# Attention tail of a fused two-layer kernel: a second level of Strassen's rule for four of seven value products, a moved transpose, and one accumulator tile in the MLP

## Chip, core and metric

The kernel runs on one core of one Trainium2 chip, in float32, as one launch. The metric is the device time of that launch in microseconds (us). The core has five engines with queues of their own, each of which works strictly through its queue: TensorE (PE in the profile, with its weight loads as PEld), VectorE (DVE), ScalarE (ACT), GpSimd (POOL) and SyncE (SP, which here only issues DMAs).

## What is computed

The reference chains two layers on x of shape (2, 512, 32, 32), that is two batches of 512 channels by 1024 positions.

```python
# layer 0: deformable attention (with a small MLP as position bias), then, for each batch
x = x + out_proj(attention) + out_b
h1 = gelu(mlp_w1 @ bn2(x) + mlp_b1)            # 512 -> 2048 channels
x = x + mlp_w2 @ h1 + mlp_b2                   # 2048 -> 512 channels
# layer 1: plain attention over the 1024 positions, one head of 512 channels
q, k, v = Wq @ x + bq, Wk @ x + bk, Wv @ x + bv
attn = softmax(q.T @ k / sqrt(512))            # 1024 x 1024
out = x + Wp @ (v @ attn.T) + bp
```

The change lies in the MLP of layer 0 (one tile) and at the end of layer 1.

## The kernel before

**Strassen's rule.** All large products are block products with seven multiplications instead of eight. Each operand is cut in four blocks; `fold` and `spread` (lines 116 to 128, on VectorE or POOL) form three more blocks from them by sums, so that a list of seven blocks stands for each operand. `PARTS` (line 112) says which two blocks each of the products 1 to 7 multiplies. `multiply` (line 130) takes a PSUM tile (128 x 2 x 512) for each product, lets TensorE fill it, and calls a function that takes it out of PSUM: a copy on ScalarE, or a sum on VectorE (`plus`, line 136, all of whose instructions carry the line L137).

**A second level.** `twice` (lines 141 to 178) does two of these products at once, each by seven half-sized steps: it is used in the first layer of the MLP. The order of its steps is written out by hand (`STEPS`, line 139: place in the order, number of the step); set g is shifted by 7 g places, and other work can be put in between as "fills", with a place of its own. In each step both products of the set write halves of one PSUM bank. Steps 1, 6, 7, 4 share a bank and add up in it, each after ScalarE has copied the state before out; step 2 has a bank in a second tile, whose other bank takes steps 5 and 3. VectorE takes steps 2, 5 and 3 out.

**PSUM.** In the MLP and the tail, `mq` deals four PSUM tiles in turn (line 1151). A product therefore can begin when the product four tiles earlier has been taken out.

**Stages.** Up to about 1900 us the kernel works through the position bias (L697 and what belongs to it). Then come the output projection, the MLP, and layer 1. The MLP has eight units (line 1152): batch 0 and 1, and in each four slices of the 2048 hidden channels. A unit is `layer1` (line 1056), with gelu on ScalarE, and `layer2` (line 1100), with seven products in the order 2, 1, 3, 5, 6, 7, 4. Products 1, 5, 6, 7 are collected over the four units of a batch in a tile `acc` of four quarters (line 1103): the first unit copies them there on ScalarE (L1108), the others add on VectorE. A new `acc` is taken for each batch from a pool that has room for one. `finish(b)` (line 1120) adds the four quarters to x in eight VectorE sums; that of batch 0 is issued behind layer 1 of batch 1's first unit (lines 1165 to 1167).

**The tail, layer 1.** It runs over the two batches (line 1196). Weights are merged beforehand: gg for q and k, gn for v and Wp together, loaded and folded on POOL by `load_g` (line 907); gn is loaded once, ahead of the loop. For each batch: seven products form q (line 1225), 2 x 7 form the scores of two halves u of the queries (`scores`, line 1249), each followed by a softmax. `turn(u, e)` (line 1272) transposes a half by 32 TensorE transposes, four ScalarE copies into aT (L1281), and three VectorE sums. Seven products `turned` (line 1295) form the transposed values vt. Seven products of vt by aT (line 1368, order 1, 2, 6, 7, 5, 3, 4, eight matmuls of 128 x 512 each) give the output; their results are added to x on VectorE, and each finished quarter is stored by two SP DMAs of 256 KB (L1331, L1366). The order on TensorE is: turn(0), the seven products for vt, turn(1), the seven products of vt by aT. At the end of the VectorE work on vt, `blocks(b + 1)` (line 924) prepares the next batch's x in four sums.

Instructions of all helpers carry the helper's line: L1201 are the matmuls of q, the scores and the value-times-attention products, L1299 those of vt, L1040 those of the MLP's plain products, L159 those of `twice`.

Of the kernel before, what the change touches and what calls it, by code (L numbers as in the profile page):

```python
# [8 lines left out]
F32 = mybir.dt.float32  # L9
AF = mybir.ActivationFunctionType  # L10
ALU = mybir.AluOpType
# [46 lines left out]
def conv_seq_kernel(ctx: ExitStack, tc: tile.TileContext, x, xt, kst, pst, cst, vec, wsm, outw, w1, w2, wl, wlt, brow, out):  # L58
# [79 lines left out]

    STEPS = ((0, 1), (1, 2), (3, 6), (4, 5), (6, 7), (9, 4), (12, 3))

    def twice(pool, sets, weights, moving, dest, done, fills=()):
        todo = [(7 * g + t, g, q) for g in range(len(sets)) for t, q in STEPS]
        todo += [(t, None, fill) for t, fill in fills]
        held = {}
        for _, g, q in sorted(todo, key=lambda e: e[0]):
            with tc.issue_after(newest(mybir.EngineType.PE)):
                if g is None:
                    q()
                    continue
                if q == 1:  # L150
                    held[g] = pool.tile([P, 2, 512], F32, tag="ps2", name="sw")
                if q == 2:
                    held[g, 2] = pool.tile([P, 2, 512], F32, tag="ps2", name="sw")
                bank = {2: lambda: held[g, 2][:, 0], 5: lambda: held[g, 2][:, 1], 3: lambda: held[g, 2][:, 1]}.get(
                    q, lambda: held[g][:, 0]
                )().rearrange("p (e n) -> p e n", e=2)
                s, t = PARTS[q]
                for e, p in enumerate(sets[g]):
                    nc.tensor.matmul(  # L159
                        bank[:, e, :], weights(p, s), moving(p, t), start=(q in (1, 2, 5) and e == 0), stop=True,  # L160
                        skip_group_check=True,
                    )
            d11, d12, d21, d22 = (dest(g, m, h) for m in range(2) for h in range(2))
            if q == 1:
                nc.scalar.copy(d11, bank)  # L165
            elif q == 2:
                plus(d11, d11, bank)
            elif q == 6:
                nc.scalar.copy(d12, bank)
            elif q == 7:  # L170
                nc.scalar.activation(d22, bank, AF.Copy, scale=-1.0)
                b5 = held[g, 2][:, 1].rearrange("p (e n) -> p e n", e=2)
                plus(d22, d22, b5, ALU.subtract)
            elif q == 4:
                nc.scalar.activation(d21, bank, AF.Copy, scale=-1.0)
            elif q == 3:
                plus(d12, d12, bank)
                done(g)
# [756 lines left out]
    with ExitStack() as top, tc.tile_pool(name="wp", bufs=1) as wp:  # L935
        halves = [(b, h) for b in range(B) for h in range(2)]
        units = [(b, p) for b in range(B) for p in range(NU)]
        wts, accs, copied = {}, {}, []

        def gather(w):  # L940
            for o, v in ((4, 2), (3, 0), (5, 4), (6, 5)):
# [114 lines left out]
        def layer1(p, we, w, xb, xe, hm, others=()):  # L1056
            def gelu(blk, src, scale=1.0):
                for m in range(2):
                    nc.scalar.activation(
                        hm[:, blk, m, :], src[:, m, :], AF.Gelu,  # L1060
                        bias=col("mb1", 4 * p + 2 * (blk // 2) + m), scale=scale,
                    )

            c11, c12, c21, c22, r5, r3 = (hm[:, j] for j in range(6))

            def weights(q, j):
                a = FIRST_W[PARTS[q][0]]
                return inner_w(w, we, a, a - 1)[j]

            def moving(q, j):  # L1070
                b_ = FIRST_X[PARTS[q][1]]
                return inner_x(xb, xe, b_, b_ - 1)[j]

            def dest(g, m, h):
                return hm[:, 2 * g : 2 * g + 2, m, 256 * h : 256 * h + 256]

            def done(g):
                if g == 0:
                    plus(c12, c12, c11)
                elif g == 1:  # L1080
                    plus(c22, c22, c12)
                    plus(c21, c21, c22)
                    gelu(2, c21, -1.0)
                else:
                    plus(c22, c22, r5)
                    gelu(3, c22, -1.0)
                    plus(c12, c12, r5)
                    plus(c12, c12, r3)
                    gelu(1, c12)

            def second():
                ps = mq.tile([P, 2, 512], F32, tag="ps2", name="sw")
                product(w, xb)(ps, 0, 0)
                plus(c11, c11, ps)
                gelu(0, c11)

            twice(mq, ((1, 6), (4, 7), (5, 3)), weights, moving, dest, done, ((21, second), *others))
            spread([hm[:, j] for j in range(7)])

        def layer2(b, p, w, hm):  # L1100

            if p == 0:
                accs[b] = mp.tile([P, 4, 2, 512], F32, tag="acc", name="acc")

            def own(j):
                a = accs[b][:, j]
                if p == 0:
                    return lambda ps: nc.scalar.copy(a, ps)  # L1108
                return lambda ps: plus(a, a, ps)

            def give(o2, h, op):
                x_ = xs[:, 2 * o2 : 2 * o2 + 2, b, h * 512 : (h + 1) * 512]
                return lambda ps: plus(x_, x_, ps, op)

            multiply(mq, (2, 1, 3, 5, 6, 7, 4), product(w, hm), {
                1: own(0), 5: own(1), 6: own(2), 7: own(3),
                2: give(0, 0, ALU.add), 3: give(0, 1, ALU.add), 4: give(1, 0, ALU.subtract),
            })

        def finish(b):  # L1120
            p1, p5, p6, p7 = (accs[b][:, j] for j in range(4))
            for o in range(NCH):
                nc.scalar.activation(xs[:, o, b, :], xs[:, o, b, :], AF.Identity, bias=col("mb2", o))
            v = [xs[:, o2 : o2 + 2, b, n : n + 512] for o2 in (0, 2) for n in (0, 512)]
# [19 lines left out]
        spread(op1[1])  # L1144
        project(1, *op1, op1w[:, 3:5].rearrange("p a k n -> p a (k n)"))
        xe, part = sums(xb)
        load_second(0)


# [40 lines left out]
    SC = float(C) ** (-0.5)  # L1190
    outv = out.rearrange("b (k p) n -> p k b n", p=P)
    with tc.tile_pool(name="sp", bufs=1) as sp:
        gn = sp.tile([P, 7, 2, 256], F32, name="gn")
        load_g(gn, 1)

        for b in range(B):
            def product(w, x, c=0, nk=2):
                def go(ps, a, b_):
                    for m in range(2):
# [72 lines left out]
            def turn(u, e):  # L1272
# [10 lines left out]
                            ps.rearrange("p a (c n) -> p a c n", n=P),  # L1283
                        )
                n = slice(256 * u, 256 * u + 256)
                spread([aT[:, j, :, n] for j in range(6)], range(3))

            e0 = scores(0)
            e1 = scores(1)
# [15 lines left out]
                return lambda ps: f(ps.rearrange("p a n -> p (a n)"))  # L1305

            def v5(ps):
                plus(vf[2], vf[2], ps, ALU.subtract)
                plus(vf[1], vf[1], ps)

            multiply(mq, (1, 6, 7, 4, 5, 3, 2), turned, {p: flat_(f) for p, f in {
                1: lambda ps: nc.scalar.copy(vf[0], ps), 6: lambda ps: plus(vf[1], vf[0], ps),
                7: lambda ps: nc.vector.scalar_tensor_tensor(vf[2], ps, -1.0, vf[1], ALU.mult, ALU.subtract),
                4: lambda ps: plus(vf[3], vf[2], ps, ALU.subtract), 5: v5,
                3: lambda ps: plus(vf[1], vf[1], ps), 2: lambda ps: plus(vf[0], vf[0], ps),
            }.items()})
            fold(nc.vector, vf)
            turn(1, e1)
            if b + 1 < B:
                xbl = blocks(b + 1)  # L1320


            x11, x12, x21, x22 = (xs[:, o : o + 2, b, n : n + 512] for o in (0, 2) for n in (0, 512))
            tv = sp.tile([P, 2, 512], F32, name="tv")
            for o in range(NCH):
                nc.scalar.activation(xs[:, o, b, :], xs[:, o, b, :], AF.Identity, bias=ub[:, 1, o : o + 1])

# [2 lines left out]
                for o in (2 * o2, 2 * o2 + 1):  # L1330
                    nc.sync.dma_start(out=outv[:, o, b, n], in_=xs[:, o, b, n])  # L1331

            def a1(ps):
                nc.scalar.copy(tv, ps)
                plus(x11, x11, ps)

            def a2(ps):
                plus(x11, x11, ps)
                store(0, 0)

            at = [aT[:, j] for j in (0, 1, 2, 3, 4, 5, 5)]

            def a6(ps):
                plus(tv, tv, ps)
                plus(x12, x12, tv)
                nc.vector.scalar_tensor_tensor(at[6], at[5], -1.0, at[2], ALU.mult, ALU.subtract)

            def a7(ps):
                plus(tv, tv, ps)
                plus(x22, x22, tv, ALU.subtract)  # L1350
                plus(x21, x21, tv, ALU.subtract)

            def a5(ps):
                plus(x22, x22, ps, ALU.subtract)
                store(1, 1)
                plus(x12, x12, ps)

            def a3(ps):
                plus(x12, x12, ps)
                store(0, 1)  # L1360

            def a4(ps):
                for m in range(2):
                    x_ = xs[:, 2 + m, b, 0:512]
                    plus(x_, x_, ps[:, m, :], ALU.subtract)
                    nc.sync.dma_start(out=outv[:, 2 + m, b, 0:512], in_=x_)  # L1366

            multiply(mq, (1, 2, 6, 7, 5, 3, 4), product(vt, at, nk=4), {
                1: a1, 2: a2, 6: a6, 7: a7, 5: a5, 3: a3, 4: a4,
            })  # L1370


def _constants(np):
# [113 lines left out]
```

## Time and profile before

| | |
|---|---|
| median of 3 runs | 2631.12 us (2630.61 to 2632.42) |
| the profiled execution | 2630.3 us, of which the profile's span is 2628.5 |
| granted TensorE clock, mean | 0.999 |
| TensorE, VectorE, ScalarE, POOL busy | 99%, 87%, 66%, 30% of the span |
| MLP, first step of `twice` to its last product | 1945.7 to 2319.6 us of the span |
| tail, batch 0 and batch 1 | 2319.6 to 2471.4, 2471.4 to 2628.5 us |
| last matmul's end, end of the span | 2623.3, 2628.5 us |

How to read the profile: a row of groups names line, engine, operation, output and input tiles, shape and count, then busy time and the mean duration of one in ns, then the idle time of the engine ahead of it and who ended it. A timeline row has the start and the duration of one instruction or of a run of equal ones (us), then engine, line, operation, tiles, count, and in brackets the idle time ahead of it. A float32 matmul is two MATMUL records. Starts of equal matmuls in a row are closer than their durations, since they are pipelined.

### The profile page before, as it was taken

How to read it: one execution, taken by the hardware profiler on the slowest of the kernel's cores; microseconds unless marked ns; L12 is line 12 of the kernel's file. 1: busy time of each engine (PE TensorE's matmuls, PEld its weight loads, DVE VectorE, ACT ScalarE, POOL GpSimd, SP SyncE). 2: the span in 40 equal slices, each digit the busy share in tenths (PEclk: the TensorE clock that was granted, in tenths of full speed). 3: DMA queues.
4: the chain of work that ended last, by engine and by line, in shares of the span. 5: the costliest groups of instructions: out<-in, count | busy, mean ns of one | idle time of the engine just before them, and what ended most of it. 6: DMA issues, size and time to landing. Idle time of an engine off the chain costs nothing.

```text
span 2628.5 us, 47874 instructions
## 1 busy us (share of the span) xinstructions
PE 2611.6 (99%) x19656; PEld 1005.9 (38%) x19656; DVE 2281.3 (87%) x1425; ACT 1742.8 (66%) x2311; POOL 798.3 (30%) x899
## 2 busy tenths in 40 slices
PE   9999999999999999999999999999999999999999
PEld 3333332333233333333333333333355655646454
DVE  7999999999999999999999999999785685666354
ACT  5887898878888878887887777777632242315041
POOL 1333333333333333333333333333333333200000
PEclk9999999999999999999999999999999999999999
DMA  5788878888877888888887888888777677300000
GB/s 190 177 176 183 188 167 173 184 181 195 176 172 170 180 177 197 175 176 173 174 185 168 183 172 173 179 176 178 172 189 159 143 169 160 71 16 0 32 1 32
DMA packets 164809, 403.52 MB, mean 154 GB/s; under 512 B 24784, under 2 KB 72032, under 8 KB 161904
## 3 DMA queue, kind: packets, MB, share of 16 engines
q0 software_dynamic: 99104, 256.29, 53.7%
q1 hardware_dynamic: 65056, 143.88, 15.6%
q8 instruction: 155, 2.54, 0.4%
q14 instruction: 62, 0.51, 0.1%
q10 hardware_dynamic: 432, 0.31, 0.0%
HBM read 81.10 MB, written 6.55 MB: 33 GB/s over the span
## 4 chain that ended last, share of the span: by engine, by line
PE 93%; DVE 3%; ACT 2%; issue 1%; DMA 0%; DVEq 0%; ACTq 0%
PE ps L697 65%; PE sw L1201 9%; PE sw L1040 6%; PE sw L159 5%; PE sw L987 2%; PE sw L1299 2%; PE sim L783 1%; PE psg L599 1%; DVE hm L137 1%; ACT rx L706 0%; DVE xs L137 0%; ACT ub L708 0%; PE pkv L533 0%; PE sim L766 0%; PE pt L800 0%
## 5 line engine op out<-in xcount | busy, mean ns | idle before, releaser
L697 PE MATMUL ps<-h,cw 128*32 128x512 f32 x16384 | 1776.3, 592 | 3.8 <-ACT rx L706 2.8
L680 DVE CUSTOM_DVE_ANT_1 h<-ta,tb 128x4096 f32<-128x4096 f32 (+1 forms) x257 | 1131.0, 4402 | 29.3 <-PE ps L697 26.4
L697 PEld LDWEIGHTS ps<-h,cw 128*32 128x32 f32 x16384 | 541.9, 110 | 1202.7 <-issue 1137.0
L706 ACT ACTIVATE rx<-ps,sc 128x1024 f32<-128x1024 f32 x512 | 568.0, 1109 | 145.4 <-PE ps L697 126.3
L708 ACT ACTIVATE ub<-ps,sc 128x1024 f32<-128x1024 f32 x256 | 308.2, 1204 | 92.9 <-PE ps L697 92.7
L716 DVE SCALAR_TENSOR_TENSOR ub<-rx,sc,ub 128x1024 f32<-128x1024 f32 x256 | 327.0, 1277 | 6.6 <-ACT ub L708 6.6
L735 POOL DMA_DIRECT2D ua<-uc x126 | 155.3, 1244 | 318.5 <-DMA ua<-uc 311.7
L735 POOL DMA_DIRECT2D ua<-ua x189 | 219.9, 1322 | 27.0 <-DMA ua<-uo 20.2
L1040 PE MATMUL sw<-hm,w2t 128*128 128x512 f32 x448 | 195.8, 597 | 3.9 <-ACT acc L1108 3.7
L718 POOL DMA_DIRECT2D uo<-ub x127 | 124.2, 978 | 223.5 <-DVE ub L716 208.9
L708 ACT ACTIVATE uo<-ps,sc 128x1024 f32<-128x1024 f32 x128 | 154.2, 1205 | 51.1 <-PE ps L697 50.7
L716 DVE SCALAR_TENSOR_TENSOR uo<-rx,sc,uo 128x1024 f32<-128x1024 f32 x128 | 163.6, 1278 | 8.0 <-ACT uo L708 7.9
L735 POOL DMA_DIRECT2D uc<-uo x63 | 53.1, 842 | 332.2 <-DMA uc<-uo 332.2
L1040 PEld LDWEIGHTS sw<-hm,w2t 128*128 128x128 f32 x448 | 85.5, 191 | 109.4 <-issue 99.6
L137 DVE TENSOR_TENSOR hm<-hm,sw 128x512 f32<-128x512 f32 (+1 forms) x80 | 58.8, 738 | 71.2 <-PE sw L159 50.8
L137 DVE TENSOR_TENSOR xs<-xs,sw 128x1024 f32<-128x1024 f32 (+1 forms) x48 | 55.7, 1173 | 67.8 <-PE sw L1201 36.0
L718 POOL DMA_DIRECT2D ua<-ub x64 | 58.5, 914 | 162.8 <-DVE ub L716 153.0
L1201 PE MATMUL sw<-aT,vt 128*128 128x512 f32 x224 | 96.7, 593 | 0.3 <-ACT aT L1281 0.3
L660 ACT ACTIVATE ta<-fb,vs 128x512 f32<-128x512 f32 (+1 forms) x65 | 89.3, 1376 | 8.1 <-DMA fb<-fdr 8.1
L708 ACT ACTIVATE ua<-ps,sc 128x1024 f32<-128x1024 f32 x64 | 77.0, 1203 | 20.4 <-PE ps L697 20.1
L708 ACT ACTIVATE uc<-ps,sc 128x1024 f32<-128x1024 f32 x64 | 77.1, 1205 | 20.2 <-PE ps L697 18.9
L165 ACT COPY hm<-sw 128x512 f32<-128x512 f32 x24 | 14.1, 586 | 112.5 <-PE sw L159 112.5
(271 smaller groups left out, 2522.7 us busy)
## 6 DMA issues: line engine op xcount, KB each, us to landing
uo<-ub POOLq DMA_DIRECT2D x127, 512.0 KB, 5.5
fb<-fdr SPq DMA_DIRECT2D x64, 512.0 KB, 5.3
ua<-ub POOLq DMA_DIRECT2D x64, 512.0 KB, 6.0
uc<-ub POOLq DMA_DIRECT2D x64, 512.0 KB, 5.2
ua<-ua POOLq DMA_DIRECT2D x63, 256.0 KB, 6.2
ua<-uo SPq DMA_DIRECT2D x63, 256.0 KB, 2.3
ua<-uo POOLq DMA_DIRECT2D x63, 256.0 KB, 6.1
uc<-uc POOLq DMA_DIRECT2D x63, 256.0 KB, 7.1
```

The source lines that it names most:

```text
L137: nc.vector.tensor_tensor(out, a, b_, op)
L159: nc.tensor.matmul(bank[:, e, :], weights(p, s), moving(p, t), start=(q in (1, 2, 5) and e == 0), stop=True, skip_group_check=True,)
L660: nc.scalar.activation(ta.rearrange("p j x -> p x j")[:, :, j0:j1], fb[:, 0, :, j0:j1], AF.Identity, bias=col("cb1"), scale=col("w1x"),)
L680: nc.vector._custom_dve(TENSOR_ADD_SAT, out=h1[:, y : y + step].rearrange("p y t x -> p (y t x)"), in0=a.unsqueeze(1).to_broadcast([P, ste ...
L697: nc.tensor.matmul(ps[32 * q : 32 * q + 32, h, :], cw2[:, 32 * z : 32 * z + 32], h1[:, 16 * h : 16 * h + 16, q, :], start=True, stop=True,)
L706: nc.scalar.activation(o, ps, AF.Relu, bias=sc[:, 4 + z : 5 + z])
L708: nc.scalar.activation(o, ps, AF.Relu, bias=sc[:, 4 + z : 5 + z], scale=sc[:, z : z + 1])
L716: nc.vector.scalar_tensor_tensor(r[1], r[0], sc[:, z : z + 1], r[1], ALU.mult, ALU.add)
L718: nc.gpsimd.dma_start(out=sums[s][1], in_=sums[s][3], accum_op=ALU.add)
L735: nc.gpsimd.dma_start(out=out, in_=in_, accum_op=ALU.add)
L1040: nc.tensor.matmul(ps[:, m, :], w[:, a, k, m * P : (m + 1) * P], x[:, b_, k, :], start=(k == 0), stop=(k == 1),)
L1201: nc.tensor.matmul(ps[:, m, :], w[:, a, k, c + m * P : c + (m + 1) * P], x[b_][:, k, :], start=(k == 0), stop=(k == nk - 1),)
```

## The change

1. In the MLP, one tile acc is taken ahead of the loop and used for both batches.
2. In the tail, turn(1) moves to between the third and the fourth product of vt; the order of these products changes, and with it some signs.
3. Of the seven value-times-attention products, 1 and 6 (set 0) and 7 and 5 (set 1) go through `twice`, which can now take several matmuls per step (two, along the contraction) and a sign. Its results stand in tiles rs. Products 2, 3, 4 stay whole and are fills. New are the sums for the half-sized blocks (x_sums, w_sums) in tiles x45, oe, ow6, and the places where they are made: set 0's within and behind the products of vt, set 1's in a fill.
4. One sum of each `turn` is made later, for both halves at once (third). `blocks(b + 1)` moves into the fill with set 1's sums.
5. x11 and x12 receive set results by accumulating DMAs on POOL's queue (give), in place of VectorE sums; stores of these quarters wait for them.
6. gn shares its space with oe, so it is loaded and folded again for batch 1.

```diff
@@ -138,7 +138,7 @@
     STEPS = ((0, 1), (1, 2), (3, 6), (4, 5), (6, 7), (9, 4), (12, 3))
-    def twice(pool, sets, weights, moving, dest, done, fills=()):
+    def twice(pool, sets, weights, moving, dest, done, fills=(), sign=-1.0):
         todo = [(7 * g + t, g, q) for g in range(len(sets)) for t, q in STEPS]
         todo += [(t, None, fill) for t, fill in fills]
         held = {}
@@ -156,10 +156,11 @@
                 )().rearrange("p (e n) -> p e n", e=2)
                 s, t = PARTS[q]
                 for e, p in enumerate(sets[g]):
-                    nc.tensor.matmul(
-                        bank[:, e, :], weights(p, s), moving(p, t), start=(q in (1, 2, 5) and e == 0), stop=True,
-                        skip_group_check=True,
-                    )
+                    for k, (w, x) in enumerate(zip(weights(p, s), moving(p, t))):
+                        nc.tensor.matmul(
+                            bank[:, e, :], w, x, start=(q in (1, 2, 5) and e == k == 0), stop=True,
+                            skip_group_check=True,
+                        )
             d11, d12, d21, d22 = (dest(g, m, h) for m in range(2) for h in range(2))
             if q == 1:
                 nc.scalar.copy(d11, bank)
@@ -168,11 +169,11 @@
             elif q == 6:
                 nc.scalar.copy(d12, bank)
             elif q == 7:
-                nc.scalar.activation(d22, bank, AF.Copy, scale=-1.0)
+                nc.scalar.activation(d22, bank, AF.Copy, scale=sign)
                 b5 = held[g, 2][:, 1].rearrange("p (e n) -> p e n", e=2)
-                plus(d22, d22, b5, ALU.subtract)
+                plus(d22, d22, b5, ALU.subtract if sign < 0 else ALU.add)
             elif q == 4:
-                nc.scalar.activation(d21, bank, AF.Copy, scale=-1.0)
+                nc.scalar.activation(d21, bank, AF.Copy, scale=sign)
             elif q == 3:
                 plus(d12, d12, bank)
                 done(g)
@@ -1099,11 +1100,8 @@
         def layer2(b, p, w, hm):
-            if p == 0:
-                accs[b] = mp.tile([P, 4, 2, 512], F32, tag="acc", name="acc")
-
             def own(j):
-                a = accs[b][:, j]
+                a = acc[:, j]
                 if p == 0:
                     return lambda ps: nc.scalar.copy(a, ps)
                 return lambda ps: plus(a, a, ps)
@@ -1118,7 +1116,7 @@
             })
         def finish(b):
-            p1, p5, p6, p7 = (accs[b][:, j] for j in range(4))
+            p1, p5, p6, p7 = (acc[:, j] for j in range(4))
             for o in range(NCH):
                 nc.scalar.activation(xs[:, o, b, :], xs[:, o, b, :], AF.Identity, bias=col("mb2", o))
             v = [xs[:, o2 : o2 + 2, b, n : n + 512] for o2 in (0, 2) for n in (0, 512)]
@@ -1144,6 +1142,7 @@
         spread(op1[1])
         project(1, *op1, op1w[:, 3:5].rearrange("p a k n -> p a (k n)"))
         xe, part = sums(xb)
+        acc = mp.tile([P, 4, 2, 512], F32, name="acc")
         load_second(0)
@@ -1190,10 +1189,10 @@
     SC = float(C) ** (-0.5)
     outv = out.rearrange("b (k p) n -> p k b n", p=P)
     with tc.tile_pool(name="sp", bufs=1) as sp:
-        gn = sp.tile([P, 7, 2, 256], F32, name="gn")
-        load_g(gn, 1)
-
         for b in range(B):
+            gn = sp.tile([P, 7, 2, 256], F32, name="gn")
+            load_g(gn, 1)
+
             def product(w, x, c=0, nk=2):
                 def go(ps, a, b_):
                     for m in range(2):
@@ -1283,7 +1282,7 @@
                             ps.rearrange("p a (c n) -> p a c n", n=P),
                         )
                 n = slice(256 * u, 256 * u + 256)
-                spread([aT[:, j, :, n] for j in range(6)], range(3))
+                spread([aT[:, j, :, n] for j in range(6)], range(2))
             e0 = scores(0)
             e1 = scores(1)
@@ -1305,23 +1304,54 @@
                 return lambda ps: f(ps.rearrange("p a n -> p (a n)"))
             def v5(ps):
-                plus(vf[2], vf[2], ps, ALU.subtract)
+                plus(vf[2], vf[3], ps)
                 plus(vf[1], vf[1], ps)
-            multiply(mq, (1, 6, 7, 4, 5, 3, 2), turned, {p: flat_(f) for p, f in {
+            took = {p: flat_(f) for p, f in {
                 1: lambda ps: nc.scalar.copy(vf[0], ps), 6: lambda ps: plus(vf[1], vf[0], ps),
-                7: lambda ps: nc.vector.scalar_tensor_tensor(vf[2], ps, -1.0, vf[1], ALU.mult, ALU.subtract),
-                4: lambda ps: plus(vf[3], vf[2], ps, ALU.subtract), 5: v5,
-                3: lambda ps: plus(vf[1], vf[1], ps), 2: lambda ps: plus(vf[0], vf[0], ps),
-            }.items()})
+                7: lambda ps: plus(vf[3], vf[1], ps), 5: v5, 3: lambda ps: plus(vf[1], vf[1], ps),
+                4: lambda ps: plus(vf[3], vf[3], ps), 2: lambda ps: plus(vf[0], vf[0], ps),
+            }.items()}
+            multiply(mq, (1, 6, 7), turned, took)
+            turn(1, e1)
+
+            sets = ((1, 6), (7, 5))
+            where = {p: (g, e) for g, pair in enumerate(sets) for e, p in enumerate(pair)}
+            x45 = [sp.tile([P, 2, 2, 2, 256], F32, tag="e0", name="x45", bufs=2) for _ in sets]
+            rs = [sp.tile([P, 2, 2, 512], F32, tag="e1", name="rs", bufs=2) for _ in sets]
+            inner = {}
+
+            def ax(g, at):
+                at_ = (slice(0, 6, 5), slice(1, 5, 3))[g] if at is None else at
+                return [aT[:, at_, 2 * k : 2 * k + 2, 256 * n : 256 * n + 256] for k, n in AT_X]
+
+            def wx(g, at):
+                at_ = (slice(0, 6, 5), slice(3, 5))[g] if at is None else at
+                return [vt[:, at_, 2 * k : 2 * k + 2, P * n : P * n + P] for k, n in AT_W]
+
+            def x_sums(g):
+                x = ax(g, None) + [x45[g][:, 0], x45[g][:, 1], inner["x"][g]]
+                for o, u, v in ((4, 1, 0), (5, 3, 4), (1, 3, 1), (6, 2, 5)):
+                    plus(x[o], x[u], x[v], ALU.subtract)
+
+            def w_sums(g):
+                w = wx(g, None) + inner["w"][g]
+                plus(w[4], w[3], w[2])
+                for o, u, v in ((5, 4, 0), (6, 1, 5), (3, 0, 3)):
+                    plus(w[o], w[u], w[v], ALU.subtract)
+
+            multiply(mq, (5, 3, 4, 2), turned, took)
+            oe = sp.tile([P, 14, 256], F32, tag="gn", name="oe")
+            inner["x"] = [oe[:, 4 * i : 4 * i + 4, :].rearrange("p (e k) n -> p e k n", e=2) for i in range(2)]
+            ow = oe[:, 8:14, :].rearrange("p a n -> p (a n)").rearrange("p (j e k n) -> p j e k n", j=3, e=2, k=2)
+            ow6 = sp.tile([P, 2, 2, P], F32, name="ow6")
+            inner["w"] = [[ow[:, 0], ow[:, 1], w6] for w6 in (ow[:, 2], ow6)]
+            x_sums(0)
             fold(nc.vector, vf)
-            turn(1, e1)
-            if b + 1 < B:
-                xbl = blocks(b + 1)
+            w_sums(0)
             x11, x12, x21, x22 = (xs[:, o : o + 2, b, n : n + 512] for o in (0, 2) for n in (0, 512))
-            tv = sp.tile([P, 2, 512], F32, name="tv")
             for o in range(NCH):
                 nc.scalar.activation(xs[:, o, b, :], xs[:, o, b, :], AF.Identity, bias=ub[:, 1, o : o + 1])
@@ -1330,44 +1360,74 @@
                 for o in (2 * o2, 2 * o2 + 1):
                     nc.sync.dma_start(out=outv[:, o, b, n], in_=xs[:, o, b, n])
-            def a1(ps):
-                nc.scalar.copy(tv, ps)
-                plus(x11, x11, ps)
-
-            def a2(ps):
-                plus(x11, x11, ps)
-                store(0, 0)
-
-            at = [aT[:, j] for j in (0, 1, 2, 3, 4, 5, 5)]
-
-            def a6(ps):
-                plus(tv, tv, ps)
-                plus(x12, x12, tv)
-                nc.vector.scalar_tensor_tensor(at[6], at[5], -1.0, at[2], ALU.mult, ALU.subtract)
-
-            def a7(ps):
-                plus(tv, tv, ps)
-                plus(x22, x22, tv, ALU.subtract)
-                plus(x21, x21, tv, ALU.subtract)
-
-            def a5(ps):
-                plus(x22, x22, ps, ALU.subtract)
-                store(1, 1)
-                plus(x12, x12, ps)
-
-            def a3(ps):
-                plus(x12, x12, ps)
-                store(0, 1)
+            def give(out, r):
+                nc.gpsimd.dma_start(out=out, in_=r, accum_op=ALU.add)
+
+            r1, r6, r7, r5 = (rs[g][:, e] for g in range(2) for e in range(2))
+
+            def weights(p, j):
+                g, e = where[p]
+                w = wx(g, PARTS[p][0])[j] if j < 4 else inner["w"][g][j - 4][:, e]
+                return [w[:, k] for k in range(2)]
+
+            def moving(p, j):
+                g, e = where[p]
+                x = ax(g, PARTS[p][1])[j] if j < 4 else (x45[g][:, 0], x45[g][:, 1], inner["x"][g])[j - 4][:, e]
+                return [x[:, k] for k in range(2)]
+
+            def done(g):
+                if g == 0:
+                    give(x11, r1)
+                    store(0, 0)
+                    plus(r6, r6, r1)
+                    give(x12, r6)
+                    last = aT[:, 5]
+                    a, c = (aT[:, 5, k : k + 2, 256:512] for k in (0, 2))
+                    plus(a, c, a, ALU.subtract)
+                    nc.vector.scalar_tensor_tensor(last, last, -1.0, aT[:, 2], ALU.mult, ALU.subtract)
+                else:
+                    give(x12, r5)
+                    store(0, 1)
+                    plus(r7, r7, r6)
+                    plus(x21, x21, r7)
+                    plus(x22, x22, r5)
+                    plus(x22, x22, r7)
+                    store(1, 1)
+
+            whole = product(vt, [aT[:, j] for j in (0, 1, 2, 3, 4, 5, 5)], nk=4)
+
+            def plain(p, took):
+                def go():
+                    ps = mq.tile([P, 2, 512], F32, tag="ps2", name="sw")
+                    whole(ps, *PARTS[p])
+                    took(ps)
+                return go
             def a4(ps):
                 for m in range(2):
                     x_ = xs[:, 2 + m, b, 0:512]
-                    plus(x_, x_, ps[:, m, :], ALU.subtract)
+                    plus(x_, x_, ps[:, m, :])
                     nc.sync.dma_start(out=outv[:, 2 + m, b, 0:512], in_=x_)
-            multiply(mq, (1, 2, 6, 7, 5, 3, 4), product(vt, at, nk=4), {
-                1: a1, 2: a2, 6: a6, 7: a7, 5: a5, 3: a3, 4: a4,
-            })
+            def third():
+                with tc.issue_after(newest(mybir.EngineType.DVE)):
+                    spread([aT[:, j] for j in range(6)], (2,))
+
+            def second():
+                nonlocal xbl
+                x_sums(1)
+                w_sums(1)
+                if b + 1 < B:
+                    with tc.issue_after(newest(mybir.EngineType.DVE)):
+                        xbl = blocks(b + 1)
+
+            twice(mq, sets, weights, moving, lambda g, m, h: rs[g][:, :, m, 256 * h : 256 * h + 256], done, (
+                (-1, plain(2, lambda ps: plus(x11, x11, ps))),
+                (-2, third),
+                (6.5, second),
+                (15, plain(3, lambda ps: plus(x12, x12, ps))),
+                (20, plain(4, a4)),
+            ), 1.0)
 def _constants(np):
```

The built order on TensorE behind the products of vt is, in each batch: product 2; set 0's steps 1, 2, 6, 5, 7; set 1's steps 1, 2; set 0's step 4; set 1's steps 6, 5; set 0's step 3; set 1's step 7; product 3; set 1's steps 4, 3; product 4. A step is four matmuls of 128 x 256.

More of the change, by code (lines that the diff above doesn't have):

```diff
@@ L937, in conv_seq_kernel @@
         units = [(b, p) for b in range(B) for p in range(NU)]
-        wts, accs, copied = {}, {}, []
+        wts, copied = {}, []
         def gather(w):
@@ L1067, in weights @@
                 a = FIRST_W[PARTS[q][0]]
-                return inner_w(w, we, a, a - 1)[j]
+                return [inner_w(w, we, a, a - 1)[j]]
             def moving(q, j):
                 b_ = FIRST_X[PARTS[q][1]]
-                return inner_x(xb, xe, b_, b_ - 1)[j]
+                return [inner_x(xb, xe, b_, b_ - 1)[j]]
             def dest(g, m, h):
```

## The prediction

> **What bounds the kernel now.** I read the page first: its span, its busy shares and its chain. TensorE (PE) is busy for 99% of the span and carries 93% of the chain.
>
> ```profile
> span 2628.5 us, 47874 instructions
> PE 2611.6 (99%) x19656; PEld 1005.9 (38%) x19656; DVE 2281.3 (87%) x1425; ACT 1742.8 (66%) x2311; POOL 798.3 (30%) x899
> ...
> PE 93%; DVE 3%; ACT 2%; issue 1%; DMA 0%; DVEq 0%; ACTq 0%
> ```
>
> So time is won by fewer matmul columns or by closing gaps between matmuls. All gaps of PE together are 2628.5 - 2611.6 = 16.9 us, 5.2 us of them the tail after the last matmul. Next, PE's waits:
>
> ```profile
> PE sw L1040 <- ACT acc L1108: 3.7, 1, 3.7
> ...
> PE sw L1201 <- ACT aT L1281: 0.3, 2, 0.2
> ```
>
> The largest is one wait of 3.7 us in the MLP's second layer, first unit of batch 1. The timeline there shows the cause: ScalarE's copies into acc (L1108) wait until VectorE (DVE) has ended the whole of finish(0), though the PSUM tiles had long been full. The windows (us: PE, weight loads, DVE, ACT, POOL; granted clock, DMA share, GB/s) show a second price, a slow clock for over 5 us afterwards.
>
> ```profile
> 2161.89 1.22 DVE L137 TENSOR_TENSOR acc<-acc 128x1024 f32<-128x1024 f32 x1
> 2163.03 1.22 DVE L137 TENSOR_TENSOR xs<-xs,acc 128x1024 f32<-128x1024 f32 x1
> ...
> 2167.57 3.49 DVE L137 TENSOR_TENSOR xs<-xs,acc 128x1024 f32<-128x1024 f32 x3
> ...
> 2171.59 1.22 DVE L137 TENSOR_TENSOR xs<-xs,sw 128x1024 f32<-128x1024 f32 x1
> ```
> ```profile
> 2171.15 2.84 ACT L1108 COPY acc<-sw 128x1024 f32<-128x1024 f32 x3 [13.96 <-DVE xs L137]
> ```
> ```profile
> 2172.22 8.83 PE L1040 MATMUL sw<-hm,w2t 128*128 128x512 f32 x16 [3.68 <-ACT acc L1108]
> ```
> ```profile
> 2172.00:2174.00 2.00, 1.78 (x3) 0.82 (x4) 0.81 (x1) 1.99 (x3) 2.00 (x3) 0.77 0.50 144
> 2174.00:2176.00 2.00, 2.00 (x4) 0.86 (x3) 0.00 (x0) 0.00 (x0) 0.61 (x1) 0.50 1.34 158
> 2176.00:2178.00 2.00, 2.00 (x6) 0.84 (x5) 0.00 (x0) 0.35 (x1) 0.00 (x0) 0.87 1.18 185
> 2178.00:2180.00 2.00, 2.00 (x6) 0.83 (x5) 0.00 (x0) 0.66 (x1) 0.85 (x1) 1.00 0.60 102
> ```
>
> Last, the attention tail's timeline of batch 0 (batch 1 is alike): PE runs without a gap but for 0.16 us, and the seven value-times-attention products are one row. A source matmul is two MATMUL records.
>
> ```profile
> 2412.48 7.07 PE L1299 MATMUL sw<-gn,xs 128*128 128x256 f32 x32
> 2419.39 3.66 PE L1277 MATMUL psx<-ident,e 128*128 128x128 f32 x32
> 2423.21 48.33 PE L1201 MATMUL sw<-aT,vt 128*128 128x512 f32 x112 [0.16 <-ACT aT L1281]
> ```
>
> **Part 1: matmuls saved.** By start times a 512-column record costs 48.33/112 = 0.432 us, and a 256-column one (2419.39-2412.48)/32 = 0.216 us: halves cost half. Products 1, 6, 7, 5 go from 4 x 16 = 64 records of 512 columns (27.6 us) to 2 sets x 7 steps x 8 = 112 records of 256 (24.2 us). Saved: 3.4 us a batch, **6.9 us**.
>
> **Part 2: the turn moved between the value products.** Its 32 transposes (3.66 us) and four copies are the same. It now starts after three value products, at 2395.21 + 10.4 = 2405.6; ScalarE normalised that half at 2403.3 (end of L1246's row), so 2.3 us of cover remain. Without them it would wait. The 0.16 us gap per batch, the wait for aT's last copy, lies under four value products afterwards: 0.3 us won. Against it speaks "TensorE: Matmul & The Clock Gate", Part 4: PE-mode transpose, which says transposes do not count as PE activity for the clock gate. By it, 3.66 us of transposes would let the following matmuls run slow (about 1.8 us, as in part 5, per batch). But the windows of 2419 to 2424 and 2424 to 2472 granted 1.00 right behind such a block. I take the row: nothing.
>
> **Part 3: VectorE's new sums.** Rows: a back-to-back 128x1024 sum takes 1.135 us (2163.03-2161.89), 2048 elements 2.2 (L1346), 512 elements 0.60 back to back (0.69 alone, also for MLP operands cut in the same blocks). Per batch are added 8 input sums of 1024 (9.1 us) and 8 weight sums and one restoring sum of 512 (5.4); eight sums of 1024 that took the four products (9.1) become six evictions of 512 (4.1) and five sums of 1024 (5.7). DVE was 20 us busy of 48 here; it gets 15 more, most of them early, so its order decides. PE must not write step 5 of a set before DVE has taken step 2 (the built program has this wait). Take 0 as the end of the last value product on PE.
> - DVE until it has taken set 0's step 2: 0.3 latency + 5 x 1.135 (last value eviction, one input sum, three folds) + 4 x 0.60 + 2.2 (the deferred aT sum) + 1.135 (product 2) + 0.69 = 12.4. PE until step 5: product 2 (6.9) + three steps of 8 x 0.216 = 1.72: 12.0. PE waits 0.4 us, in each batch.
> - DVE on to set 1's step 2: 4 x 1.135 + 0.60 + 5 x 0.60, in batch 0 also 3 x 1.135 for blocks(1), moved ahead of it, + 0.69: 24.6 in batch 0, 21.2 in batch 1. PE is at 12.4 + 6 x 1.72 = 22.7 by then: it waits 1.9 us in batch 0, none in batch 1.
> Sum: 0.4 + 1.9 + 0.4 = **2.7 us lost**. A gap of 0.8 us at 2097 left the clock at 1.00, that of 3.68 us did not; I charge none for 1.9. Bounds: nothing lost if DVE is 5% quicker than these rows, about 10 lost if its sums take the 1.416 us that some took beside POOL (rival C).
>
> ScalarE gets eight copies of 0.59 us in place of one of 1.0, beside idle time: nothing. With the gn tile shared, batch 1 reloads gn (4 DMAs, 4.1 us to landing, 4 POOL sums of 1.27). On SP these stand ahead of batch 0's last stores, which nobody awaits; on POOL behind three accumulating DMAs; the reader is a value product some 75 us later. Nothing; without that cover, 9 us.
>
> **Part 4: accumulating DMAs on the path of the end.** x12 gets its last term by a POOL DMA of 512 KB. Count from E, the end of PE. Set 1's step 3 ends at E-6.9; DVE takes it by E-5.9 (ahead of it product 3's addition waits for the earlier DMA, issued after set 0's step 3: E-18.9 + 0.3 + 0.6 + 2.2 + 1.2 = E-14.6, landed at E-9.1, so it is through before). The same rows in the main loop land 5.5 us after issue (uo<-ub). "DMA: Bandwidth & Descriptors", Anatomy of one DMA, gives about 2 us plus size at 436 GB/s, 3.2 us here; that would hide it. I take the row: landed at E-0.3. SP waits for it, and behind it on SP queue x22's and x21's stores: six of 256 KB. Stores took 0.69 us each of all 16 engines (4.8% of 229 us over 16) and landed after 2.1: 1.4 + 6 x 0.69 = 5.5 us. Then 1.7 us to the end, as now. So E + 6.9; now it is 5.2: **1.7 us lost**. Bounds: 0 if it lands in 4.5 us, 5.5 lost if in 8 (then product 3's addition waits too, so landing counts twice).
>
> **Part 5: one acc tile.** The first copy now needs only the second of finish(0)'s eight operations (built waits), done at 2164.25, so PSUM is free before 2168.54 and the 3.68 us go. Next late is product 3's addition on DVE, 2171.59 + 1.22 = 2172.87, for product 4, wanted at 2168.54 + 3.43 = 2171.97: 0.9 us. Now layer 1 starts at 2180.88; then at 2172.87 + 3.43 = 2176.3. **Gain 4.6 us**: 2.8 of gap and 1.8 of clock (8.66 us from start to next start for 16 records of 0.43). Bounds: 0, if others wait for DVE too, and 5.5, if product 4 need not wait.
>
> **Sum.** -6.9 - 0.3 + 2.7 + 1.7 - 4.6 = -7.4 us. The profiled execution took 2630.3 (span 2628.5) and would take 2622.9; the median of the runs is 0.8 above it: **2623.7 us**.
>
> **Rivals.**
> - A, all is hidden: DVE keeps up and the DMA lands in time: -6.9 - 0.3 - 4.6 = -11.8, 2619.3. For it: estimates of 0.4 to 1.9 us are near nothing. Against: DVE has no idle time in my count. 10%.
> - B, a half is lost: the MLP gap turns into other waits behind DVE (nothing of 4.6 won, 2628.3), or DMAs land in 8 us (2627.5). For: queues landed as late as 10.6 us; against: the DMA engines were about 80% busy, and are nearly idle here. 18%, about 2628.
> - C, slower: DVE becomes the bound of both value stages. Where POOL computes beside it, its 1024 sums averaged 1.416 us instead of 1.22. If its chained work in a batch (about 12 us ahead of my zero and 24.6 behind) stretches by s, batch 0 waits s longer and batch 1 s - 1.5, and a gap like that of 3.7 us costs 1.8 of clock. It eats the 7.4 us from s = 3.5 (10% slower sums); at s = 6 it adds 10.5 + 1.8: 2636. Against: POOL computes nothing there, and the same shapes took 1.22 and 0.69. 7%.
> - The change does what it says: the built order has the new steps and the finer waits.
>
> **How the numbers follow.** A measurement can tell about 0.2%, 5.3 us. My forecast (2621 to 2626) has 65%. Faster by over 5.3 us is below 2625.9: the forecast but for its upper edge, and A, 0.75. Within: B and that edge, 0.18. Slower: C, 0.07. Range 2619.5 to 2628.5, from A's sum to the middle of B.
>
> **What would show it.** In the changed profile: 224 records of 256 columns in the new steps at 0.216 us; PE's waits for DVE's rs sums near 0.4, 1.9, 0.4 us; the L1108 wait gone, a wait of about 0.9 for xs in its place, and the clock at 1.00 there; from the last matmul to the end 6.9 us. I am wrong if DVE's sums take longer than these rows, if PE waits elsewhere (a transpose for the softmax), or if the accumulating DMAs land much later.

## The result, and the profile after

The changed kernel takes 2621.46 us (median of 6 runs, 2620.61 to 2622.24), the kernel before 2631.03 us (6 runs): a ratio of 0.9963, 95% interval 0.9952 to 0.9974. The profiled execution took 2621.26 us.

The page after, its span, busy shares and chain:

```profile
span 2619.2 us, 48156 instructions
...
PE 2603.7 (99%) x19752; PEld 1030.5 (39%) x19752; DVE 2313.2 (88%) x1463; ACT 1750.4 (67%) x2325; POOL 814.1 (31%) x909
...
PE 91%; DVE 4%; ACT 2%; issue 2%; DMA 1%; DVEq 0%; POOL 0%; ACTq 0%; POOLq 0%; SPq 0%
```

PE lost 7.9 us of busy time and stays the bound. DVE is 31.9 us busier, and its share of the chain rises from 3 to 4%: it is where the new waits are. Of PE's waits for sw, the PSUM tiles of the MLP and the tail, these two rows come to over 0.2 us:

```profile
PE sw L160 <- DVE rs L137: 2.2, 3, 1.6
...
PE sw L1041 <- DVE hm L125: 0.7, 1, 0.7
```

The 3.7 us wait for the copies into acc has gone, and three waits for DVE's evictions into rs (its taking of results out of PSUM) have come. (The last row stands at 0.2 in every other profile, so I count it as scatter.) Where the time went, by starts in the two timelines:

| point | before, us | after, us | gained so far |
|---|---|---|---|
| layer 2 of batch 1's first MLP unit starts | 2151.21 | 2151.43 | -0.2 |
| the layer 1 behind it starts | 2180.88 | 2175.46 | 5.4 |
| tail starts | 2319.62 | 2313.96 | 5.7 |
| turn(0) of batch 0 starts | 2391.72 | 2386.06 | 5.7 |
| batch 1 starts | 2471.38 | 2464.46 | 6.9 |
| last matmul ends | 2623.30 | 2613.20 | 10.1 |
| span ends | 2628.5 | 2619.2 | 9.3 |

So the MLP unit gave 5.6 us, batch 0's tail 1.3, batch 1's 3.2, and the end took 0.8 back; the 0.2 us left over, in the rest of the MLP, is not explained.

**The MLP.** PE's timeline after has all 56 records of that layer 2 in one row without a gap (before: 40, a gap, 16). ScalarE's copies run one by one instead of all at the end, and DVE's row at 2171.81 ends at 2173.03:

```profile
2151.43 24.20 PE L1041 MATMUL sw<-hm,w2t 128*128 128x512 f32 x56
...
2164.56 1.01 ACT L1106 COPY acc<-sw 128x1024 f32<-128x1024 f32 x1 [7.15 <-DVE xs L137]
...
2171.81 1.22 DVE L137 TENSOR_TENSOR xs<-xs,sw 128x1024 f32<-128x1024 f32 x1
```

In the windows over the same place the clock (third number from the end) is 1.00, where it was 0.77 and 0.50:

```profile
2172.00:2174.00 2.00, 2.00 (x6) 0.95 (x5) 1.03 (x1) 1.01 (x1) 2.00 (x3) 1.00 0.38 107
2174.00:2176.00 2.00, 2.00 (x7) 1.05 (x6) 0.34 (x1) 0.00 (x0) 0.68 (x1) 1.00 1.36 183
```

**The tail of batch 0.** PE and DVE around the two sets:

```profile
2427.55 1.89 PE L160 MATMUL sw<-x,oe 128*128 128x256 f32 x8
2429.71 1.99 PE L160 MATMUL sw<-x,oe 128*128 128x256 f32 x8 [0.27 <-DVE rs L137]
2431.54 5.34 PE L160 MATMUL sw<-aT,vt 128*128 128x256 f32 x24
2436.72 1.89 PE L160 MATMUL sw<-oe,vt 128*128 128x256 f32 x8
2438.45 1.89 PE L160 MATMUL sw<-x,oe 128*128 128x256 f32 x8
2441.99 1.99 PE L160 MATMUL sw<-x,oe 128*128 128x256 f32 x8 [1.65 <-DVE rs L137]
2443.82 1.89 PE L160 MATMUL sw<-aT,oe 128*128 128x256 f32 x8
```
```profile
2438.99 1.21 DVE L932 TENSOR_TENSOR tx<-xs 128x1024 f32<-128x1024 f32 x1
2440.12 1.22 DVE L931 SCALAR_TENSOR_TENSOR tx<-tx,xs 128x1024 f32<-128x1024 f32 x1
2441.26 0.68 DVE L137 TENSOR_TENSOR rs<-rs,sw 128x512 f32<-128x512 f32 x1
```

A step without a wait starts 1.73 us behind the one before (2436.72 - 2431.54 = 5.18 us for three steps). The step with the 0.27 us wait starts 2.16 us behind, and the next 1.83 us behind it. So a wait named 0.27 costs 0.43 + 0.10 = 0.53 us, and the one named 1.65 costs 3.54 - 1.73 + 0.10 = 1.91: each 0.26 more than its name, 0.16 because the name counts from the end of a row that lasts 1.89 us, not 1.73, and 0.10 in the step behind the wait. The DVE rows show the cause of the second: the eviction of set 1's step 2, which PE had ended by 2436.9, stands behind three of the block sums for the next batch (L930, L932, L931).

**The end.** POOL, SP, DVE and SP again, with 2613.20 as the last matmul's end (2606.17 + 7.03):

```profile
2607.61 1.19 POOL L1364 DMA_DIRECT2D xs<-rs  x1 [7.76 <-DVE rs L137]
...
2612.63 1.79 SPq L1361 DMA_DIRECT2D out<-xs  x4
2613.24 1.28 DVE L137 TENSOR_TENSOR xs<-xs,sw 128x512 f32<-128x512 f32 x2 [1.44 <-PE sw L1200]
2614.52 1.20 SPq L1410 DMA_DIRECT2D out<-xs  x2
```

The DMA for r5 was issued at 2607.61; SP gets on at 2612.63, 5.0 us later, issues four stores, and only then the last two.

### The profile page after: what moved, and what is told of

The parts are those of the page before. It is cut to its first block, busy times and chain, and to the rows that moved or that the text cites. A ratio compares the mean times of both kernels' runs of the same rounds, so it can differ in the third digit from the quotient of the medians.

```text
span 2619.2 us, 48156 instructions
## 1 busy us (share of the span) xinstructions
PE 2603.7 (99%) x19752; PEld 1030.5 (39%) x19752; DVE 2313.2 (88%) x1463; ACT 1750.4 (67%) x2325; POOL 814.1 (31%) x909
## 4 chain that ended last, share of the span: by engine, by line
PE 91%; DVE 4%; ACT 2%; issue 2%; DMA 1%; DVEq 0%; POOL 0%; ACTq 0%; POOLq 0%; SPq 0%
PE ps L698 63%; PE sw L1041 7%; PE sw L1200 7%; PE sw L160 6%; PE sw L988 2%; PE sw L1298 2%; PE sim L784 1%; PE psg L600 1%; DVE hm L137 1%; PE psx L1276 1%; ACT rx L707 1%; DVE ub L717 0%; DVE h L681 0%; PE pkv L534 0%; DVE oe L137 0%
## 5 line engine op out<-in xcount | busy, mean ns | idle before, releaser
L698 PEld LDWEIGHTS ps<-h,cw 128*32 128x32 f32 x16384 | 549.0, 110 | 1195.8 <-issue 1123.4
L1364 POOL DMA_DIRECT2D xs<-rs x6 | 7.2, 1195 | 261.4 <-DVE rs L137 261.4
L717 DVE SCALAR_TENSOR_TENSOR uc<-rx,sc,uc 128x1024 f32<-128x1024 f32 x64 | 81.8, 1278 | 2.7 <-ACT uc L709 2.5
```

Of the source, the lines that this page charges most:

```text
L698: nc.tensor.matmul(ps[32 * q : 32 * q + 32, h, :], cw2[:, 32 * z : 32 * z + 32], h1[:, 16 * h : 16 * h + 16, q, :], start=True, stop=True,)
L717: nc.vector.scalar_tensor_tensor(r[1], r[0], sc[:, z : z + 1], r[1], ALU.mult, ALU.add)
```

## The experiments

### The MLP tile alone, and the value part alone

e1 is the kernel before with the one-tile edit; e2 the changed kernel with that edit undone.

```diff
         def layer2(b, p, w, hm):
...
-            if p == 0:
-                accs[b] = mp.tile([P, 4, 2, 512], F32, tag="acc", name="acc")
...
         xe, part = sums(xb)
+        acc = mp.tile([P, 4, 2, 512], F32, name="acc")
```

> The kernel before with one change: one acc tile for both batches; all seven value products stay plain. Theory (from the profile after): the whole 3.68 us wait and its clock price go, and no new wait comes, so the first MLP unit of batch 1 takes from its first layer-2 matmul to the next layer 1 24.0 us in place of 29.7: -5.6 us, 2625.4 us. Rival 1 (the prediction's own part 5): product 4 still waits 0.9 us for product 3's addition: -4.6 us, 2626.4, with a PE wait for xs of 0.9 us in the trace. Rival 2: the gain comes only together with the value part, and the gap turns into other waits behind DVE: -1 us or less, 2630.

> The changed kernel with acc again one tile per batch: the value part alone. Theory: parts add up, so it is 5.6 us slower than the changed kernel and about 3.7 us faster than the kernel before: 2627.3 us, with the 3.7 us wait for the copies into acc (L1108 before) back at batch 1's first unit and the clock below 1.00 behind it. Rival: the two parts interact (the value part alone gives nothing): 2631.

Measured: e1 2624.57 us (11 runs) beside 2630.43 for the kernel before, ratio 0.9976 (0.9968 to 0.9985), so 5.9 us faster. PE's rows of the unit in e1, then in e2:

```profile
2152.12 24.20 PE L1040 MATMUL sw<-hm,w2t 128*128 128x512 f32 x56
2176.16 1.89 PE L159 MATMUL sw<-xb,w1t 128*128 128x256 f32 x8
```
```profile
2172.18 8.83 PE L1041 MATMUL sw<-hm,w2t 128*128 128x512 f32 x16 [3.68 <-ACT acc L1108]
```

In e1 the unit takes 2176.16 - 2152.12 = 24.04 us, and no wait for xs is in the trace. e2 took 2626.97 us (20 runs), ratio 0.9986 (0.9979 to 0.9993), 3.5 us faster; its unit takes 2180.85 - 2151.17 = 29.68 us with the wait of 3.7 us back. Within the noise the parts add up (0.24% and 0.14% beside 0.37% together). Three fifths of the gain come from the one tile, not from the second level of products.

### The second turn behind all value products

```diff
-            multiply(mq, (1, 6, 7), turned, took)
+            multiply(mq, (1, 6, 7, 5, 3, 4, 2), turned, took)
             turn(1, e1)
...
-            multiply(mq, (5, 3, 4, 2), turned, took)
```

> The changed kernel with the second half's turn put back behind all seven value products. Theory: DVE's sums for set 0 then start behind the last aT copy, 13.8 us later than now, but DVE can fold the values while it waits. Its work from the first aT sum (about 2419.1 us on the clock of the changed kernel's batch 0) to the eviction of set 0's step 2 is 7 x 1.135 + 3 x 0.60 + 2.2 = 11.9 us: the eviction starts at 2431.05 in place of 2428.97, so PE waits about 2.35 us at set 0's step 5 in place of 0.27, in both batches: +4.2 us on the changed kernel, about 2625.7. Rival 1: the place of the turn is worth only its cover for the last copy: +0.3 us. Rival 2: a gap of 2.35 us also costs clock as the 3.68 us gap did: up to +1.8 us more in each batch, 2629.

Measured: 2625.02 us, one run. PE's timeline:

```profile
2427.03 1.89 PE L160 MATMUL sw<-x,oe 128*128 128x256 f32 x8
2431.11 1.99 PE L160 MATMUL sw<-x,oe 128*128 128x256 f32 x8 [2.19 <-DVE rs L137]
2432.94 5.34 PE L160 MATMUL sw<-aT,vt 128*128 128x256 f32 x24
```

The step starts 4.08 - 1.73 = 2.35 us late, in both batches, and the wait for aT's last copy (0.17 and 0.16) is back. The step behind the wait takes 1.83 us, as behind a wait of 0.27: a gap of that size costs no clock (the windows from 2420 to 2468 all grant 1.00). By stages (start of turn(0) to start of batch 1: 80.74 us for 78.40; from there to product 4's start: 144.06 for 141.71) the move is worth 4.7 us, not 0.3. It makes DVE's sums early enough for the sets; without it the second level wins nothing over e1, with its seven plain products: from turn(0) of batch 0 to the end of the span e5 takes 2622.9 - 2385.11 = 237.8 us, e1 2623.1 - 2386.29 = 236.8 (whole runs: 2625.02 beside 2624.57).

### Three more sums on DVE's chain

```diff
             def second():
                 nonlocal xbl
+                for _ in range(3):
+                    plus(x45[1][:, 0], ax(1, None)[1], ax(1, None)[0], ALU.subtract)
                 x_sums(1)
```

> The changed kernel with DVE's first input sum of set 1 done four times in place of once (the same values again, nothing else changes): three more sums of 1.135 us ahead of the eviction of set 1's step 2, of which one restoring sum of 0.60 us has moved away in the built order: 2.8 us more DVE work on that chain. Theory: DVE sets the time there, so PE's wait of 1.65 us in batch 0 becomes 4.45 us, and in batch 1, where 1.6 us of slack are seen, a wait of 1.2 us comes up: +4.0 us, 2625.4, if a gap of 4.45 us costs no clock, and +5.8 us, 2627.2, if it costs the 1.8 us that the gap of 3.68 us in the MLP of the kernel before did. I take the second. Rival: DVE's order is not what PE waits for: +0 us.

Measured: 2627.13 us, one run. PE's timeline in batch 0 (in batch 1 the new wait is 1.05 us) and the windows there:

```profile
2438.65 1.89 PE L160 MATMUL sw<-x,oe 128*128 128x256 f32 x8
2444.99 3.53 PE L160 MATMUL sw<-x,oe 128*128 128x256 f32 x8 [4.45 <-DVE rs L137]
2448.35 1.89 PE L160 MATMUL sw<-aT,oe 128*128 128x256 f32 x8
```
```profile
2444.00:2446.00 2.00, 1.01 (x2) 0.84 (x3) 2.00 (x4) 0.00 (x0) 0.00 (x0) 0.68 0.00 0
2446.00:2448.00 2.00, 2.00 (x6) 1.64 (x5) 0.67 (x2) 0.00 (x0) 0.00 (x0) 0.50 0.03 8
2448.00:2450.00 2.00, 2.00 (x10) 1.71 (x10) 0.00 (x0) 0.00 (x0) 0.00 (x0) 0.97 0.00 0
```

The wait grew by 2.8 us, the whole added work; so DVE sets the time there. The eight records behind it take 3.36 us instead of 1.83: the clock had dropped, for 1.5 us more. This is rival C's mechanism in small: it exists. By stages, 2.8 us of DVE work per batch cost 4.3 us in batch 0 (first set's step 6 to batch 1: 41.24 us for 36.91) and 1.3 in batch 1 (step 6 to product 4: 29.44 for 28.13). It did not decide in the changed kernel, because the sums on DVE's chain kept the durations of the prediction's rows (1.22 and 0.68 us above).

### The three waits taken away, one by one

e3 puts blocks(b + 1) in a fill of its own at place 8.5, behind set 1's step 2 (place 8); e4 lets DVE add r5; e7 does both and moves third:

```diff
-                    give(x12, r5)
+                    plus(x12, x12, r5)
...
-                (-2, third),
+                (1.5, third),
                 (6.5, second),
+                (8.5, fourth),
```

> The changed kernel with blocks(1) as a step of its own behind set 1's step 2, so that in DVE's order the eviction of that step comes ahead of three of the four block sums. Theory: PE's wait of 1.65 us in batch 0 goes and nothing takes its place (the next eviction, of set 0's step 3, stands behind the blocks and is wanted no earlier than they end): -1.65 us on the changed kernel, a span of 2617.5 us; PE's waits for rs are 0.27 and 0.27. Rival: DVE is the bound as a whole there, and the wait comes back one step later: 0.

> The changed kernel with x12's last term r5 added by DVE instead of by an accumulating DMA (two DMAs of six go, two sums of 1.135 us come). Theory: x12's stores no longer wait for a landing, so SP has issued its six stores before product 4's halves are there: from the last matmul to the end of the span 5.2 us, as in the kernel before, in place of 6.15: -0.95 us. DVE has 1.4 us idle ahead of product 4's halves, which takes the sum of 1.135. Rival: the end is set by product 4's own sums and stores, whatever SP did before: 0, 6.1 us.

> The changed kernel with three edits at once: blocks(1) behind set 1's step 2 (-1.65 us), r5 added by DVE (-0.95 us), and the deferred aT sum of 2.2 us behind the eviction of set 0's step 2 instead of ahead of it (-0.27 us in each batch). Theory: they add up to -3.1 us on the changed kernel, about 2618.3 us; no PE wait for rs is left. Rival: each wait that goes uncovers another behind DVE, and half is lost: 2620.

> The changed kernel once more, unedited, on the chip that runs the three edits, so that these two can be compared: 2621.5 us as before, with waits for rs of 0.27, 1.65 and 0.27 us.

e3: 2618.37 us, one run, span 2616.3. The span is 2.9 us below that of the changed kernel, but 1.0 us of it was there before the edit's place (the step that waits 0.27 us starts at 2428.74 instead of 2429.71), so I read the stage. From that step to the start of batch 1 it takes 2461.57 - 2428.74 = 32.83 us instead of 2464.46 - 2429.71 = 34.75: 1.92 us gained, with no wait in its place:

```profile
2437.48 3.62 PE L160 MATMUL sw<-x,oe 128*128 128x256 f32 x16
```

e4: 2619.15 us, one run, span 2617.1. Again the stage: from the start of product 4 to the end of the span 2617.1 - 2605.08 = 12.0 us, where the changed kernel takes 2619.2 - 2606.17 = 13.0. In its timeline SP's last stores follow at once on DVE's first half:

```profile
2612.14 1.28 DVE L137 TENSOR_TENSOR xs<-xs,sw 128x512 f32<-128x512 f32 x2 [0.31 <-PE sw L1200]
2612.86 0.93 SPq L1410 DMA_DIRECT2D out<-xs  x2
```

e7: 2617.00 us (5 runs, 2616.30 to 2618.14), ratio to the kernel before 0.9948 (0.9935 to 0.9962). e8, the changed kernel on the same chip: 2622.14 (5 runs, 2619.94 to 2623.53), ratio 0.9965 (0.9953 to 0.9978), its three waits unchanged. No wait for rs is left in e7; where steps 6 and 5 of set 0 and of set 1 in batch 0 had waits between them, they are one row each:

```profile
2426.61 3.62 PE L160 MATMUL sw<-x,oe 128*128 128x256 f32 x16
...
2436.97 3.62 PE L160 MATMUL sw<-x,oe 128*128 128x256 f32 x16
```

By stages e7 beats e8 by 2.4 us from turn(0) to batch 1 (75.94 for 78.38), by 0.5 from there to product 4 (141.17 for 141.71) and by 1.1 from there to the end (11.96 for 13.03), 4.0 us in all; the single edits and two waits of 0.53 us give 1.9 + 1.0 + 2 x 0.53 = 4.0 too. The medians differ by 5.1 us; the five runs of e7 all lie below the five of e8. My expectation of 3.1 was low mainly because it took the waits by name, without the 0.26 us that each costs besides.

## Why the prediction was right, step by step

The direction and the mechanisms held, and the time was inside the range, 2.2 us below the forecast. The sum was -7.4 us; by the two profiled executions (2630.3 and 2621.26) it is -9.0. With the measured terms below, -6.9 - 0.3 + 3.0 + 0.8 - 5.6 = -9.0; without the last one it is -3.4, beside e2's 3.5 us. The terms:

- **Part 1, matmuls saved: held.** A step of eight 256-column records takes 1.73 us by starts, 14 of them 24.2 us, as forecast.
- **Part 2, the moved turn: right direction, but too small a claim.** No transpose waited for the softmax (they start at 2399.92 straight behind product 7), and the 0.16 us gaps went. The rule that I had set aside (the Trainium skill, "TensorE: Matmul & The Clock Gate", Part 4: PE-mode transpose: transposes do not count as activity) would have had the matmuls behind the transposes run slow; the windows from 2398 to 2408 of the changed kernel grant 1.00 throughout. That shows what such a block costs here, nothing; as it lasts 3.49 us (2399.92 to 2403.41), and the limit for gaps lies anywhere between 2.2 and 3.7 us (last section), it does not show whether transposes count. What I gave as 0.3 us is worth 4.7 by e5, because part 3's figures had already used the early turn: that sized one edit wrongly, not the sum.
- **Part 3, DVE's sums: held.** Forecast were waits of 0.4, 1.9 and 0.4 us; the steps start 0.43, 1.81 and 0.43 us late, and with the 0.10 us behind each the loss is 3.0 us for 2.7. e3 and e6 show DVE's order as the cause from both sides. Batch 0's tail gained 1.3 us and batch 1's 3.2, against -3.4 - 0.16 + 2.3 = -1.3 and -3.4 - 0.16 + 0.4 = -3.2.
- **Part 4, the end: right mechanism, half the size.** The term that was too large is the stores' 5.5 us. The DMA landed at the last matmul's end less 0.6 us (forecast 0.3, though the prediction's own E-5.9 and 5.5 us make it 0.4), 5.0 us after issue. By the Trainium skill, "DMA: Bandwidth & Descriptors", Anatomy of one DMA, it would have been 3.2 us, an estimate from its fit, and by the prediction's reasoning hidden; e4 shows that taking it away wins 1.0 us. From the landing to the end of the span it took 2619.2 - 2612.63 = 6.6 us, not the 5.5 + 1.7 that I had added up one behind the other. The loss is 0.8 us, not 1.7.
- **Part 5, the acc tile: right mechanism, with a wait that did not come.** "Next late is product 3's addition on DVE" was wrong (and its 2171.59 + 1.22 is 2172.81, not 2172.87). That addition ended at 2173.03, later than product 4 was wanted, and product 4 did not wait. I had carried over the tile order of the kernel before, where product 4 gets product 3's PSUM tile. In the changed program it waits for ScalarE's copy of product 5, so it got that product's tile; product 3's goes to the next unit's layer 1, which starts at 2175.46. `mq` is not one ring of four: line 1151 of the kernel before takes every fourth tile from a pool of one buffer and the other three from `zp`, a pool of three (line 196), and in this unit `zp` gave its buffers out in another order than before. Why it did is not tested. Without the 0.9 us the gain is the upper bound I had named, 5.5; measured 5.6, in e1 alone as well. The slow clock was also shorter than the "over 5 us" read from windows of 2 us: windows of 1 us on the kernel before grant 0.55, 0.50, 0.50 and 0.75 from 2173 to 2177 and 1.00 around them, which is half speed for 3.4 us. Its price of 1.8 us was read from start times, so the sum is not touched.

Of the rivals, A (nothing lost at the sets and at the end) is out by the three waits; but its time of 2619.3 lay as near as mine, since it made the opposite error. B is out: in e1 the MLP's gap did not turn into another wait, and the DMA at the end landed in 5.0 us, not 8. C's mechanism, with one sum of nearly twice the length seen beside POOL (last section), is real, but this change does not bring it onto the critical path. So the direction was earned term by term, while the 2.2 us between forecast and median are the end (0.9 us too dear), the acc tile (1.0 us too small a gain), part 3 (0.3 us too cheap), and a median 0.2 us above the profiled execution where 0.8 was added.

## What to carry to other kernels

When a wait for PSUM is taken away, read from the built changed program which tile each later product gets, and do not carry the order over. Where a second engine has to keep up, look at the order on its queue and not only at its load: three block sums for the next batch, ahead of one short eviction, cost 1.9 us here and nothing one place later. Cost a wait by the starts of the instructions on both sides of it rather than by its name.

## What the runs showed of the hardware

- Gaps on PE of 1.65 and 2.19 us left the granted clock at 1.00; those of 3.68 us (before, and e2 alike) and 4.45 us (e6) were followed by half speed for about 3.4 us, by windows of 1 us, and cost 1.8 and 1.5 us. In e6 the slow stretch began before PE went on (0.86 in 2444 to 2445, PE at 2444.99), so 0.3 us of it fell into the gap. So for these gaps the limit lies between 2.2 and 3.7 us; the idle window of about 3.4 us that the Trainium skill states ("TensorE: Matmul & The Clock Gate", Part 1: The HAM clock gate) lies in that bracket.
- An accumulating DMA of 512 KB between tiles landed 5.0 to 5.4 us after issue (six of them, median 5.1), hardly sooner than the 5.5 us in the main loop, where the DMA engines were about 80% busy. No queue stood ahead of the last one: the engines were idle from 2605.0 to 2607.6, and then 0.86 busy at 148 GB/s from 2610.0 to 2612.7. So about 3.0 of its 5.0 us were its own transfer.
- Of six equal DVE sums (xs<-xs,rs) five took 1.22 us and one 2.29 us: that one ran while POOL folded gn for the next batch (2461.94 to 2467.86). No matmul waited for it.
